# Edge layer of a four-layer network: VectorE's rows as max(c, -a) + a, and 8 of every 14 rows summed by TensorE in PSUM

## The chip, the cores and the metric

The kernel runs on one core of a Trainium2 chip. The metric is device time in microseconds (us); the median of three runs of the kernel before was 13131.24 us (13127.69 to 13149.08). The mean granted TensorE clock is read from the profile of each run, where 1.00 is full speed.

## The reference, cut to what matters

The program normalises and passes four samples through four residual layers: attention and an MLP, an edge layer, a spectral operator block, a convolution. The change concerns the second.

```python
def _L1_conv_ref(x, We, be, Wn, bn):        # x: [4 samples, 56 rows l, 56 n, 128 channels]
    W1, W2 = (We[:, :f], We[:, f:])
    proj_i = jnp.einsum('blnf,of->blno', x, W1)
    proj_j = jnp.einsum('blnf,of->blno', x, W2)
    edge = jax.nn.relu(proj_i[:, :, :, None, :] + proj_j[:, :, None, :, :] + be)
    edge_sum = edge.sum(axis=3)
    node_in = jnp.concatenate([x, edge_sum], axis=-1)
    node = jax.nn.relu(jnp.einsum('blnc,oc->blno', node_in, Wn) + bn)
    return node
# ...
x = x + _L1_conv_ref(_gn(x), We, be, Wn, bn)
```

With a = W1 n + be and c = W2 m, each row l needs a table of 56 x 56 = 3136 values relu(a[n] + c[m]) in each of 128 channels, summed over m. Everything is fp32.

## The kernel before

Channels lie on the partitions. Tiles lie in on-chip memory: in SBUF or, where TensorE's results go, in PSUM. A block is 8 rows; GpSimd builds the tables of the odd rows, VectorE those of the even ones, ScalarE applies the ReLU, and VectorE sums every row. VectorE takes c from PSUM (`pj3`), GpSimd from SBUF.

```python
        for j in range(NBLK):                       # 7 blocks of 8 rows
            # ... matmuls with W1 and W2; a = W1 xg + be and c = W2 xg go to SBUF, pj keeps c in PSUM
            pj3 = pj[:, :NB].rearrange("p (l n) -> p l n", l=8)
            for l in range(8):
                e = wk.tile([P, HH, HH], F32, name="e_e", bufs=4)
                if l % 2:
                    nc.gpsimd.tensor_add(e, bc(a[:, l, :], 2, HH), bc(c[:, l, :], 1, HH))
                else:
                    nc.vector.tensor_add(e, bc(a[:, l, :], 2, HH), bc(pj3[:, l, :], 1, HH))
                nc.scalar.activation(e, e, AF.Relu)
                nc.vector.tensor_reduce(es_[:, 8 * j + l, :], e, AX.X, ALU.add)
            # ... po = Wn[0] xg + Wn[1] es_ in PSUM; o = relu(po + bn) on ScalarE
            nc.vector.tensor_add(xf[:, blk(j)], xf[:, blk(j)], o)
```

`bc(t, axis, n)` repeats t n times along a new axis. After the edge layer, each sample is stored to memory (`x2d`), and the spectral layer loads it again as `s_x`, transposed. The first work of the spectral layer on a loaded sample is a group norm, then `s_xn`.

Of the kernel before, what the change touches and what calls it, by code (L numbers as in the profile page):

```python
# [11 lines left out]
F32 = mybir.dt.float32  # L12
# [19 lines left out]
def bc(ap, axis, n):  # L32
    """ap with a new axis of n repeats."""
    ap = ap.unsqueeze(axis)
    shape = list(ap.shape)
    shape[axis] = n
    return ap.to_broadcast(shape)
# [6 lines left out]
class Env:  # L44
    """What every phase shares: the context and the constants that stay on chip."""


def host_constants():
    """Constants of the shapes alone."""
# [33 lines left out]
def l0_host(i):  # L83
    """Layer 0's weights, laid out."""
# [32 lines left out]
def window_order(x):  # L117
    """[B, 56, 56, C] -> [B, C, 3136], tokens of the shifted windows one after another."""
    x = np.roll(x, (-3, -3), (1, 2)).reshape(B, 8, 7, 8, 7, P)
    return x.transpose(0, 5, 1, 3, 2, 4).reshape(B, P, TOK)  # L120


def group_norm_stats(k, pool, psum, xt, tag):
    """Mean and 1/sqrt(var + eps) of xt [128, 3136]'s groups of 4 partitions, as [128, 1] each."""
# [25 lines left out]
def layer_norm(k, pool, psum, src, dst, g, be):  # L150
    """Layer norm over the partitions (channels) of src [128, 3136] into dst."""
# [22 lines left out]
def evac(k, i, out, ps, bias):  # L174
    """PSUM plus a per-partition bias to SBUF, on ScalarE or VectorE by turns."""
# [13 lines left out]
def window_attention(k, w, xw, xf):  # L189
    """Attention inside the 7x7 windows of the normed xw [128, 3136] (window order) -> xf."""  # L190
# [64 lines left out]
def global_attention(k, w, xf):  # L255
    """xf += attention over all tokens of layer_norm(xf), xf [128, 3136]."""
    nc, tc = k.nc, k.tc
    scale = 1.0 / math.sqrt(32.0)
    with ExitStack() as es:
# [6 lines left out]
        # Head 2p + i has rows 64i .. 64i + 31 of ka[:, p] and qa[:, p, i]; row 64i + 32 is 1 in ka, the  # L266
        # shift in qa. qa's other rows are 0, so that a matmul takes both heads' rows and keeps one's.
# [14 lines left out]
        # 32 columns of a head's values, then 32 of ones, which add up the softmax's denominator.  # L282
# [54 lines left out]
def mlp(k, w, xf, xw, x1):  # L337
    """x1 (image order) = xw + xf + MLP(layer_norm(xf)); xw and xf in window order."""
# [30 lines left out]
def edge_layer(k, w, x1):  # L369
    """x1 += relu(Wn [n, sum over m of relu(W1 n + W2 m + be)] + bn) on the normed rows, x1 [128, 56, 56]."""  # L370
    nc, tc = k.nc, k.tc
    xf = x1.rearrange("p l n -> p (l n)")
    with ExitStack() as es:
        big = es.enter_context(tc.tile_pool(name="e_big", bufs=1))
        wk = es.enter_context(tc.tile_pool(name="e_wk", bufs=2))
        psum = es.enter_context(tc.tile_pool(name="e_ps", bufs=2, space=PSUM))
        mr = group_norm_stats(k, wk, psum, xf, "g")
        xg = big.tile([P, TOK], F32, name="e_xg")
        apply_norm(k, xg, xf, mr)
        es_ = big.tile([P, HH, HH], F32, name="e_sum")  # L380
        esf = es_.rearrange("p l n -> p (l n)")
        for j in range(NBLK):
            pi = psum.tile([P, 512], F32, tag="pi", name="e_pi")
            nc.tensor.matmul(pi[:, :NB], w.W1, xg[:, blk(j)], start=True, stop=True)
            a = wk.tile([P, 8, HH], F32, name="e_a")
            nc.scalar.activation(a.rearrange("p l n -> p (l n)"), pi[:, :NB], AF.Identity, bias=w.be)
            pj = psum.tile([P, 512], F32, tag="pj", name="e_pj")
            nc.tensor.matmul(pj[:, :NB], w.W2, xg[:, blk(j)], start=True, stop=True)  # L388
            c = wk.tile([P, 8, HH], F32, name="e_c")
            nc.scalar.copy(c.rearrange("p l n -> p (l n)"), pj[:, :NB])  # L390
            pj3 = pj[:, :NB].rearrange("p (l n) -> p l n", l=8)
            for l in range(8):
                e = wk.tile([P, HH, HH], F32, name="e_e", bufs=4)
                if l % 2:
                    nc.gpsimd.tensor_add(e, bc(a[:, l, :], 2, HH), bc(c[:, l, :], 1, HH))  # L395
                else:
                    nc.vector.tensor_add(e, bc(a[:, l, :], 2, HH), bc(pj3[:, l, :], 1, HH))  # L397
                nc.scalar.activation(e, e, AF.Relu)  # L398
                nc.vector.tensor_reduce(es_[:, 8 * j + l, :], e, AX.X, ALU.add)  # L399
            po = psum.tile([P, 512], F32, tag="mm", name="e_po")  # L400
            nc.tensor.matmul(po[:, :NB], w.Wn[:, 0, :], xg[:, blk(j)], start=True, stop=False)
# [552 lines left out]
```

## Time and profile before

| | before |
|---|---|
| median of 3 runs | 13131.24 us |
| span of the profiled run | 13125.1 us |
| mean granted TensorE clock | 0.803 |
| one edge stage (normed rows to last output add), four of them | 304.7 us |
| of it VectorE busy | 296.4 us |
| last output add of the edge layer to first `s_xn` | 8.2 us |
| from there to the end | 3700.8 us |

The page's first part for the kernel before (engine, busy us, share of the span, instructions) shows TensorE (PE) in front and VectorE (DVE) second:

```profile
PE 9832.7 (75%) x38858; PEld 4305.4 (33%) x38858; DVE 6024.5 (46%) x5577; ACT 2924.0 (22%) x3032; POOL 2708.8 (21%) x759
```

These shares average over stages with different limits. What counts for this change is which engine is never idle inside the edge stage; the prediction reads that.

### The profile page before, as it was taken

How to read it: one execution, taken by the hardware profiler on the slowest of the kernel's cores; microseconds unless marked ns; L12 is line 12 of the kernel's file. 1: busy time of each engine (PE TensorE's matmuls, PEld its weight loads, DVE VectorE, ACT ScalarE, POOL GpSimd, SP SyncE). 2: the span in 40 equal slices, each digit the busy share in tenths (PEclk: the TensorE clock that was granted, in tenths of full speed). 3: DMA queues.
4: the chain of work that ended last, by engine and by line, in shares of the span. 5: the costliest groups of instructions: out<-in, count | busy, mean ns of one | idle time of the engine just before them, and what ended most of it. 6: DMA issues, size and time to landing. Idle time of an engine off the chain costs nothing.

```text
span 13125.1 us, 90658 instructions
## 1 busy us (share of the span) xinstructions
PE 9832.7 (75%) x38858; PEld 4305.4 (33%) x38858; DVE 6024.5 (46%) x5577; ACT 2924.0 (22%) x3032; POOL 2708.8 (21%) x759
## 2 busy tenths in 40 slices
PE   7999993599999449999963999997252277654444
PEld 3333331233333123333321333332142266643332
DVE  5515317660441667135057622604848755533333
ACT  1031235203113430321343023034410000011111
POOL 1000003200000330000024000001337788831111
PEclk8999996699999669999975999998565555555555
DMA  0000000000000000000000000000000010100000
GB/s 15 0 0 0 0 0 5 5 0 0 0 0 0 5 5 0 0 0 0 0 0 5 0 0 0 0 0 10 22 4 1 6 25 23 25 8 10 10 10 5
DMA packets 17237, 68.42 MB, mean 5 GB/s; under 512 B 8154, under 2 KB 9994, under 8 KB 14146
## 3 DMA queue, kind: packets, MB, share of 16 engines
q1 hardware_dynamic: 16834, 62.62, 1.6%
q8 instruction: 305, 5.00, 0.2%
q14 instruction: 98, 0.80, 0.0%
HBM read 49.31 MB, written 13.30 MB: 5 GB/s over the span
## 4 chain that ended last, share of the span: by engine, by line
PE 71%; DVE 19%; POOL 4%; issue 3%; ACT 3%; DMA 0%; SPq 0%; POOLq 0%; DVEq 0%; ACTq 0%
PE a_p L300 21%; PE a_ss L318 20%; PE a_po L322 11%; PE u_po L766 6%; DVE e_sum L399 6%; DVE e_e L397 3%; DVE q_q L699 2%; POOL q_q L698 1%; DVE q_a L692 1%; PE id_pw L565 1%; PE id_pv L560 1%; DVE q_a L696 1%; PE sc_ps L580 1%; PE w_pt L242 1%; PE o_pk L801 1%
## 5 line engine op out<-in xcount | busy, mean ns | idle before, releaser
L318 PE MATMUL a_ss<-a_qa,a_ka 97*112 97x448 f32 x6272 | 2760.6, 562 | 0.0
L300 PE MATMUL a_p<-a_ka,a_qa 97*112 97x448 f32 x6272 | 2714.3, 565 | 21.7 <-DVE a_mx L301 21.2
L301 DVE TENSOR_REDUCE a_mx<-a_p 112x1 f32<-112x448 f32 x3136 | 1958.9, 625 | 1005.3 <-PE a_p L300 811.2
L320 ACT ACTIVATE a_pT<-a_ss 112x896 f32<-112x896 f32 x1568 | 1437.9, 917 | 2533.5 <-PE a_ss L318 2532.2
L327 DVE RECIPROCAL a_rec<-a_po 32x448 f32<-32x448 f32 x112 | 331.2, 2957 | 3172.6 <-PE a_po L322 3170.9
L363 POOL TENSOR_TENSOR x<-xf,xw 128x343 f32<-128x343 f32 (+2 forms) x36 | 29.9, 830 | 7490.2 <-DVE xf L357 7490.2
L318 PEld LDWEIGHTS a_ss<-a_qa,a_ka 97*112 97x112 f32 x6272 | 978.3, 176 | 1716.7 <-issue 1716.7
L322 PE MATMUL a_po<-a_pT,a_va 112*64 112x448 f32 x6272 | 1536.1, 564 | 0.0
L300 PEld LDWEIGHTS a_p<-a_ka,a_qa 97*112 97x112 f32 x6272 | 856.0, 175 | 1877.2 <-DVE a_mx L301 1862.9
L766 PE MATMUL u_po<-AT,u_u 112*112 112x56 f32 x4096 | 778.7, 393 | 347.8 <-DVE u_u L763 327.3
L766 PEld LDWEIGHTS u_po<-AT,u_u 112*112 112x112 f32 x4096 | 769.4, 306 | 357.1 <-issue 336.4
L399 DVE TENSOR_REDUCE e_sum<-e_e 128x56 f32<-128x3136 f32 x224 | 749.7, 3406 | 6.7 <-ACT e_e L398 6.7
L395 POOL TENSOR_TENSOR e_e<-e_a,e_c 128x3136 f32<-128x3136 f32 x112 | 610.0, 5448 | 576.6 <-DVE e_sum L399 521.8
L398 ACT ACTIVATE e_e<-e_e 128x3136 f32<-128x3136 f32 x224 | 621.0, 2810 | 283.4 <-POOL e_e L395 187.0
L762 POOL TENSOR_TENSOR u_v<-xh,u_d 112x1792 f32<-112x1792 f32 x128 | 671.1, 5264 | 16.2 <-issue 16.2
L322 PEld LDWEIGHTS a_po<-a_pT,a_va 112*64 112x64 f32 x6272 | 312.2, 134 | 1037.2 <-ACT a_pT L320 550.3
L184 ACT COPY a_qa<-a_pr 1x448 f32<-1x448 f32 x56 | 29.4, 524 | 2785.3 <-PE a_pr L309 2785.0
L761 DVE TENSOR_TENSOR u_u<-xh,u_d 112x1792 f32<-112x1792 f32 x128 | 395.0, 3088 | 463.5 <-PE u_po L766 449.9
L388 PE MATMUL e_pj<-e_xg,t_w_W 128*128 128x448 f32 x56 | 47.7, 952 | 494.7 <-DVE e_e L397 494.7
L402 PE MATMUL e_po<-e_sum,t_w_Wn 128*128 128x448 f32 x56 | 52.1, 1033 | 471.0 <-DVE e_sum L399 471.0
L704 PE MATMUL q_pp<-q_q,c_sym 128*128 128x112 f32 x64 | 23.7, 474 | 496.6 <-DVE q_q L699 496.6
L397 DVE TENSOR_TENSOR e_e<-e_a,e_pj 128x3136 f32<-128x3136 f32 x112 | 379.2, 3408 | 16.0 <-ACT e_c L390 16.0
(271 smaller groups left out, 8115.7 us busy)
## 6 DMA issues: line engine op xcount, KB each, us to landing
u_d<-dd SPq DMA_DIRECT2D x64, 392.0 KB
xw<-in_x SPq DMA_DIRECT2D x4, 1568.0 KB
x2d<-x SPq DMA_DIRECT2D x4, 1568.0 KB
s_x<-x2d SPq DMA_DIRECT2D x4, 1568.0 KB
o_x<-x2d SPq DMA_DIRECT2D x4, 1568.0 KB
out<-v_y SPq DMA_DIRECT2D x4, 1568.0 KB
t_w_qk<-in_w_qk SPq DMA_DIRECT2D x1, 1024.0 KB
t_w_w<-in_w_w SPq DMA_DIRECT2D x2, 256.0 KB
```

The costliest lines, as they stand in the source:

```text
L300: nc.tensor.matmul(pm[:KC, :NB], qa[rows, p, i, cs], ka[rows, p, blk(j)], start=True, stop=True)
L301: nc.vector.tensor_reduce(mx7[:, c, i, j:j + 1], pm[:KC, :NB], AX.X, ALU.max)
L318: nc.tensor.matmul(ss[:, i, :NB], ka[rows, p, cs], qa[rows, p, i, blk(j)], start=True, stop=True)
L320: nc.scalar.activation(pT, ss[:, :, :NB], AF.Exp, scale=scale)
L322: nc.tensor.matmul(po[64 * i:64 * i + 64, :NB], va[:, c, 2 * p + i, :], pT[:, i, :], start=(c == 0), stop=(c == NKC - 1))
L395: nc.gpsimd.tensor_add(e, bc(a[:, l, :], 2, HH), bc(c[:, l, :], 1, HH))
L397: nc.vector.tensor_add(e, bc(a[:, l, :], 2, HH), bc(pj3[:, l, :], 1, HH))
L398: nc.scalar.activation(e, e, AF.Relu)
L399: nc.vector.tensor_reduce(es_[:, 8 * j + l, :], e, AX.X, ALU.add)
L761: nc.vector.tensor_mul(u, x, bc(d[:, :, 0, :], 2, 2))
L762: nc.gpsimd.tensor_mul(v, x, bc(d[:, :, 1, :], 2, 2))
L766: nc.tensor.matmul(po[:112, b * HH:(b + 1) * HH], u[:, hp].rearrange("p i r -> p (i r)"), st.AT[:, hp, b, :], start=(hp == 0), stop=(hp == ...
```

## The change

The identity relu(a + c) = max(c, -a) + a lets the max take over the ReLU, and the sum over m of "+ a" is 56 a, which one small matmul with -56 Wn adds (na is -a). For 8 of every 14 rows nobody sums over m: TensorE multiplies each m column of the table by Wn and accumulates all 56 in the PSUM buffer of the output. VectorE builds six of those eight rows by max, GpSimd two by subtraction; the other six rows stay as they were, but all on GpSimd. Also, -a and c are now made for a whole sample ahead of its groups of 14 rows and kept in SBUF, so that the max takes both its inputs from there. The intent is to relieve VectorE and to use TensorE, which idles in this layer.

```diff
-            for l in range(8):
-                e = wk.tile([P, HH, HH], F32, name="e_e", bufs=4)
-                ...  # add on GpSimd or VectorE, ReLU, sum
+        for g0 in range(0, HH, G):                  # G, GP, GM, MQ = 14, 8, 6, 14
+            ...
+            nc.tensor.matmul(po[:, :GP * HH], w.Wn[:, 0, :], xg[:, sa], start=True, stop=False)
+            nc.tensor.matmul(po[:, :GM * HH], w56, na...[g0 rows], start=False, stop=False)
+            for m0 in range(0, HH, MQ):
+                e8 = wk.tile([P, GP, MQ, HH], F32, name="e_e8", bufs=3)
+                for lo, hi in ((0, GM), (GM, GP)):
+                    cb = bc(c[:, rows, m0:m0 + MQ], 3, HH)
+                    nb = bc(na[:, rows, :], 2, MQ)
+                    if lo == 0:
+                        nc.vector.tensor_tensor(e8[:, lo:hi], cb, nb, ALU.max)
+                    else:
+                        nc.gpsimd.tensor_sub(e8[:, lo:hi], cb, nb)
+                        ...  # ReLU on ScalarE
+                for m in range(MQ):
+                    nc.tensor.matmul(po..., w.Wn[:, 1, :], e8[:, :, m, :], start=False, stop=(m0 + m == HH - 1))
+                for _ in range(1 if m0 % (2 * MQ) == 0 else 2):
+                    e = wk.tile([P, HH, HH], F32, name="e_e")        # two buffers
+                    nc.gpsimd.tensor_sub(e, bc(c[:, row, :], 1, HH), bc(na[:, row, :], 2, HH))
+                    ...  # ReLU, VectorE's sum
```

More of the change, by code (lines that the diff above doesn't have):

```diff
@@ L44 @@
 class Env:
+    pass
 def host_constants():
@@ L372, in edge_layer @@
     xf = x1.rearrange("p l n -> p (l n)")
+    G, GP, GM, MQ = 14, 8, 6, 14
     with ExitStack() as es:
@@ L376, in edge_layer @@
         psum = es.enter_context(tc.tile_pool(name="e_ps", bufs=2, space=PSUM))
+        w56 = wk.tile([P, P], F32, name="e_w56", bufs=1)
+        nc.vector.tensor_scalar_mul(w56, w.Wn[:, 1, :], -float(HH))
         mr = group_norm_stats(k, wk, psum, xf, "g")
@@ L379, in edge_layer @@
         apply_norm(k, xg, xf, mr)
-        es_ = big.tile([P, HH, HH], F32, name="e_sum")
-        esf = es_.rearrange("p l n -> p (l n)")
+        na = big.tile([P, HH, HH], F32, name="e_na")
+        c = big.tile([P, HH, HH], F32, name="e_c")
         for j in range(NBLK):
@@ L384, in edge_layer @@
             nc.tensor.matmul(pi[:, :NB], w.W1, xg[:, blk(j)], start=True, stop=True)
-            a = wk.tile([P, 8, HH], F32, name="e_a")
-            nc.scalar.activation(a.rearrange("p l n -> p (l n)"), pi[:, :NB], AF.Identity, bias=w.be)
-            pj = psum.tile([P, 512], F32, tag="pj", name="e_pj")
+            nc.vector.tensor_scalar(na.rearrange("p l n -> p (l n)")[:, blk(j)], pi[:, :NB], w.be, -1.0, ALU.add, ALU.mult)
+            pj = psum.tile([P, 512], F32, tag="pi", name="e_pj")
@@ L388, in edge_layer @@
             nc.tensor.matmul(pj[:, :NB], w.W2, xg[:, blk(j)], start=True, stop=True)
-            c = wk.tile([P, 8, HH], F32, name="e_c")
-            nc.scalar.copy(c.rearrange("p l n -> p (l n)"), pj[:, :NB])
-            pj3 = pj[:, :NB].rearrange("p (l n) -> p l n", l=8)
-            for l in range(8):
-                e = wk.tile([P, HH, HH], F32, name="e_e", bufs=4)
-                if l % 2:
-                    nc.gpsimd.tensor_add(e, bc(a[:, l, :], 2, HH), bc(c[:, l, :], 1, HH))
-                else:
-                    nc.vector.tensor_add(e, bc(a[:, l, :], 2, HH), bc(pj3[:, l, :], 1, HH))
-                nc.scalar.activation(e, e, AF.Relu)
-                nc.vector.tensor_reduce(es_[:, 8 * j + l, :], e, AX.X, ALU.add)
@@ L400, in edge_layer @@
-            po = psum.tile([P, 512], F32, tag="mm", name="e_po")
-            nc.tensor.matmul(po[:, :NB], w.Wn[:, 0, :], xg[:, blk(j)], start=True, stop=False)
-            nc.tensor.matmul(po[:, :NB], w.Wn[:, 1, :], esf[:, blk(j)], start=False, stop=True)
-            o = wk.tile([P, NB], F32, name="e_o")
-            nc.scalar.activation(o, po[:, :NB], AF.Relu, bias=w.bn)
-            nc.vector.tensor_add(xf[:, blk(j)], xf[:, blk(j)], o)
+            nc.scalar.copy(c.rearrange("p l n -> p (l n)")[:, blk(j)], pj[:, :NB])
@@ new lines, in edge_layer @@
+        for g0 in range(0, HH, G):
+            po = psum.tile([P, 512], F32, tag="mm", name="e_po")
+            sa = slice(g0 * HH, (g0 + GP) * HH)
+            nc.tensor.matmul(po[:, :GP * HH], w.Wn[:, 0, :], xg[:, sa], start=True, stop=False)
+            nc.tensor.matmul(po[:, :GM * HH], w56, na.rearrange("p l n -> p (l n)")[:, g0 * HH:(g0 + GM) * HH],
+                             start=False, stop=False)
+            es_ = wk.tile([P, G - GP, HH], F32, name="e_sum")
+            row = g0 + GP
+            for m0 in range(0, HH, MQ):
+                e8 = wk.tile([P, GP, MQ, HH], F32, name="e_e8", bufs=3)
+                for lo, hi in ((0, GM), (GM, GP)):
+                    rows = slice(g0 + lo, g0 + hi)
+                    cb = bc(c[:, rows, m0:m0 + MQ], 3, HH)
[4 more added lines that the diff above has]
+                        nc.gpsimd.tensor_sub(e8[:, lo:hi], cb, nb)
+                        ef = e8[:, lo:hi].rearrange("p l m n -> p (l m n)")
+                        nc.scalar.activation(ef, ef, AF.Relu)
+                for m in range(MQ):
+                    nc.tensor.matmul(po[:, :GP * HH].rearrange("p (l n) -> p l n", l=GP), w.Wn[:, 1, :], e8[:, :, m, :],
+                                     start=False, stop=(m0 + m == HH - 1))
+                for _ in range(1 if m0 % (2 * MQ) == 0 else 2):
+                    e = wk.tile([P, HH, HH], F32, name="e_e")
+                    nc.gpsimd.tensor_sub(e, bc(c[:, row, :], 1, HH), bc(na[:, row, :], 2, HH))
+                    nc.scalar.activation(e, e, AF.Relu)
+                    nc.vector.tensor_reduce(es_[:, row - g0 - GP, :], e, AX.X, ALU.add)
+                    row += 1
+            po2 = psum.tile([P, 512], F32, tag="mm", name="e_po2")
+            sb = slice((g0 + GP) * HH, (g0 + G) * HH)
+            n2 = (G - GP) * HH
+            nc.tensor.matmul(po2[:, :n2], w.Wn[:, 0, :], xg[:, sb], start=True, stop=False)
+            nc.tensor.matmul(po2[:, :n2], w.Wn[:, 1, :], es_.rearrange("p l n -> p (l n)"), start=False, stop=True)
+            for ps, s in ((po, sa), (po2, sb)):
+                n = s.stop - s.start
+                o = wk.tile([P, GP * HH], F32, name="e_o")
+                nc.scalar.activation(o[:, :n], ps[:, :n], AF.Relu, bias=w.bn)
+                nc.vector.tensor_add(xf[:, s], xf[:, s], o[:, :n])
```

## The prediction

> **What bounds the kernel now.** I read the page first, for its engine shares and its chain of waits, then the timeline of the edge layer, then every engine's busy time inside that layer. The change touches nothing else: against the kernel before, the order of instructions on every engine is the same outside the edge layer, except that some BATCH_NORM_STATS2 just ahead of it move. So the question is what the four edge stages (one per sample) are worth, and what sets their pace.
>
> ```profile
> PE 71%; DVE 19%; POOL 4%; issue 3%; ACT 3%; DMA 0%; SPq 0%; POOLq 0%; DVEq 0%; ACTq 0%
> ...
> L399 DVE TENSOR_REDUCE e_sum<-e_e 128x56 f32<-128x3136 f32 x224 | 749.7, 3406 | 6.7 <-ACT e_e L398 6.7
> L395 POOL TENSOR_TENSOR e_e<-e_a,e_c 128x3136 f32<-128x3136 f32 x112 | 610.0, 5448 | 576.6 <-DVE e_sum L399 521.8
> L398 ACT ACTIVATE e_e<-e_e 128x3136 f32<-128x3136 f32 x224 | 621.0, 2810 | 283.4 <-POOL e_e L395 187.0
> ...
> L397 DVE TENSOR_TENSOR e_e<-e_a,e_pj 128x3136 f32<-128x3136 f32 x112 | 379.2, 3408 | 16.0 <-ACT e_c L390 16.0
> ```
>
> The first line is the chain that ended last, the others are groups of the edge layer: TensorE carries 71% of the whole kernel (global attention, untouched), VectorE 19%. In the edge layer VectorE is idle for 6.7 + 16.0 us in all, while GpSimd waits 521.8 us for VectorE's sums and ScalarE 283.4 us. VectorE is the bound there. The busy times of the four stages agree (columns: stretch; its length, then busy us and instructions of PE, PEld, DVE, ACT, POOL; then the granted clock):
>
> ```profile
> 2065.10:2369.80 304.70, 45.23 (x56) 13.77 (x56) 296.42 (x91) 166.11 (x77) 152.49 (x28) 0.51 0.00 0
> ```
>
> A stage lasts 304.7 us from the normed rows to the last output add, of which VectorE is busy 296.4. Four take 1219 us, 9.3% of the 13131 us. Eight rows repeat every 42.6 us (a VectorE sum starts at 2097.48 and the same one of the next block at 2140.11), so 14 rows cost 74.6 us.
>
> **A lock between VectorE and GpSimd.** I then asked what the new VectorE instructions collide with, because the old ones took care not to: L397 reads its second input from PSUM (e_pj). Two other places show what happens when both inputs lie in SBUF. The first is the output add of the edge layer itself, the second the score stage.
>
> ```profile
> 2110.79 3.42 DVE L397 TENSOR_TENSOR e_e<-e_a,e_pj 128x3136 f32<-128x3136 f32 x1
> 2114.12 2.77 DVE L405 TENSOR_TENSOR x<-x,e_o 128x448 f32<-128x448 f32 x1
> ...
> 2110.96 5.45 POOL L395 TENSOR_TENSOR e_e<-e_a,e_c 128x3136 f32<-128x3136 f32 x1 [1.21 <-DVE e_sum L399]
> ```
> ```profile
> 9753.85 5.20 DVE L692 TENSOR_TENSOR q_a<-S,t_w_qk 128x1792 f32<-128x1792 f32 x1
> ...
> 9753.21 3.96 POOL L698 TENSOR_TENSOR q_q<-q_a,q_c 128x1792 f32<-128x1792 f32 x1 [2.15 <-DVE q_a L696]
> 9757.24 4.85 POOL L694 TENSOR_TENSOR q_c<-iS,t_w_qk 128x1792 f32<-128x1792 f32 x1
> ```
>
> L397 (one input in PSUM) runs its usual 3.4 us under a GpSimd add. L405, which takes 0.62 us alone (its minimum), takes 2.77: it ends at 2116.89, just 0.48 us after the GpSimd add ends at 2116.41. L692 takes 2.01 us alone and 5.20 here, ending 1.88 us after GpSimd's 9757.17; then GpSimd's L694 (3.19 alone) takes 4.85, waiting for VectorE in turn. So the two exclude each other for whole instructions, less some 0.14 us of overlap at each change of hands, and a VectorE instruction that is waiting gets its turn before the next GpSimd one.
>
> **What the Trainium skill says.** SBUF — State Buffer, section "Who interferes with whom", says the same: a VectorE instruction with two SBUF inputs contends with a GpSimd one that reads SBUF, the later one blocks fully, while tensor_reduce and instructions with one SBUF input do not. The trace agrees (L399 stays at 3.40 to 3.42 us under GpSimd's adds). VectorE: DVE Perf Modes, section "The TRN2 errata", gives (N+151)/0.96 ns for an fp32 tensor_tensor: 3.42 us for 3136 elements, against 3.41 measured. FP8 and Floating Point Precision, section "TensorE Precision Notes", says true fp32 takes four passes; the trace shows each matmul as two MATMUL records. TensorE: Matmul & The Clock Gate, section "What's actually happening", says that the clock is halved after an idle window of some 3.4 us and comes back after a busy one. Here the stage starts at clock 0.52 (2065.0 to 2068.8) with records 0.75 us apart, then 1.00 with records 0.375 us apart.
>
> **The change, part by part.** It works in groups of 14 rows, 16 groups in all. Per group:
>
> Removed: all seven VectorE adds (3.41 each), seven of GpSimd's, 8 of 14 sums. VectorE had 7 x 3.41 + 14 x 3.41 = 71.6 us of these two kinds.
>
> VectorE now: four max of 6 x 14 x 56 = 4704 elements, (4704+151)/0.96 = 5.06 us each (estimate from the formula; the step from 1792 at 2.01 to 3136 at 3.41 gives 5.04), 20.2 us. Six sums at 3.41 are 20.4. Two output adds at 0.62 and 0.51, 1.1. Sum 41.8, plus in the first group the evacuation of na.
>
> GpSimd: six rows at 5.445, 32.7; four subtractions of 1568 elements at 2.81 (L232 has that size, also with one operand repeated along its innermost axis), 11.2. Sum 43.9.
>
> ScalarE: 6 x 2.81 + 4 x 1.5 + two output ReLUs, some 24 us: no bound.
>
> TensorE: 56 matmuls of 448 columns, 112 records at 0.375 us warm, 42.0 us, plus some 4 for the rest: 46. A quarter of 14 matmuls is 10.5 us warm. If it starts cold, the first 3.7 us do half work, so 12.4 us. Wholly cold it would be 21.
>
> If each engine ran by itself, a group would take some 47 us. But the max now reads c and na from SBUF. GpSimd's 43.9, the max's 20.2 and the output adds' 1.1 exclude each other: 65.2 us. There are six VectorE turns per group, so 12 changes of hands at 0.14 us of overlap, minus 1.7: 63.6. I walked two groups by hand in the issue order of the changed kernel (max, sum, max, sum, sum; sub, row, sub, row, row), a waiting VectorE instruction going first. The sums fall under GpSimd's rows, two row buffers are just enough, and the lock is almost never free; I add 1.0 us for the output adds, which hold VectorE behind a row. So 64.6 us per group, against 74.6. TensorE's quarter (12.4) fits into a quarter of the group (16.1), so TensorE is not on the path except at the end.
>
> One stage: 4.0 us to the first max (as to the first add now, 2065.12 to 2069.07), 4 x 64.6 = 258.4, less 1.1 for the last adds, plus a tail. The tail is new: the last quarter's ReLU 1.5, matmuls 12.4, then ReLU and add 1.6, so 15.5. In the kernel before it is 3.2 us after the last sum. That gives 276.8 against 304.7: 27.9 saved, 111.6 in four stages. The moved statistics: six of them (3.26 us) ran after the last GpSimd add ahead of each stage, now two are left, so some 2.1 us each, 8.5 in all. Total 120 us: 13131 - 120 = 13011.
>
> **Rivals.** (a) No lock in this form, for instance because the operands repeat an element. Then TensorE or GpSimd is the bound, some 50 us per group, a stage 4 + 200 + 15.5 = 219, 343 us saved, 12780 us, faster by 2.6%. For it: the split looks balanced for this (41.8, 43.9, 46). Against: L761 and L692 have repeated operands too and are blocked. (b) GpSimd holds the lock for several instructions on end. Then VectorE's sums come late behind the max, GpSimd waits for its two row buffers some 3.4 us a quarter, and a group takes 63.6 + 4 x 3.4 = 77: a stage some 326, 13210 us. For it: GpSimd's queue is always full. Against: L692 above got its turn. (c) TensorE stays cold: 4 x 21 = 84 us per group, a stage of 350, 13310 us. For it: the clock is 0.51 over the whole stage now, and the gaps of 3.7 us are near the window. Against: a cold quarter has no gap, and the clock came back within 3.7 us of work at 2068.8.
>
> **Range and chances.** The lock's sum is firm; idle time of the lock is not. One us per group is 16 us in the whole. From 60 to 68 us per group the time goes from 12935 to 13065; with some room for (b) and (c) I take 12930 to 13090. Faster by over 2% (below 12868) needs most of rival (a): 0.08. Slower by over 2% (above 13394) needs more than any rival gives: 0.02. The rest, 0.90, is within 2%.
>
> **What would show it.** Right: the max lasts far longer than 5.06 us in the mean (8 to 10), GpSimd's subtractions last longer than 5.445 and 2.81 (their busy time near 60 us a group or more), a group repeats every 64 to 65 us, TensorE's clock in the stage lies between 0.6 and 0.9, and a tail of 15 us follows the last subtraction. Wrong: max at 5.06 and a period near 50 (rival a), GpSimd idle for VectorE's sums (rival b), matmuls back to back at 0.75 us (rival c).

## The result

| | before | after |
|---|---|---|
| median, beside each other (4 runs each) | 13129.47 us | 13093.62 us |
| range | 13101.69 to 13149.08 | 13087.71 to 13098.3 |
| profiled span | 13125.1 us | 13096.5 us |
| one edge stage (the four lie within 0.5) | 304.7 us | 281.2 to 281.6 us |
| four stages | 1219.0 us | 1125.7 us |
| last output add to first `s_xn` | 8.2 us | 23.3 us |
| first `s_xn` to the end | 3700.8 us | 3756.8 us |

The ratio is 0.9972 (95% interval 0.9958 to 0.9987): the same within 2%, and 3.6 us above the predicted range. A ratio here and below is the mean time of one kernel's fast runs over that of the other's of the same rounds, so it is not quite the ratio of the medians quoted.

The page of the kernel after: the engines' busy times, then (cut) its chain that ended last, then groups of the edge layer (busy us, mean ns of one, idle time before them and what ended it).

```profile
PE 10533.2 (80%) x40666; PEld 4687.2 (36%) x40666; DVE 5660.3 (43%) x5437; ACT 2654.9 (20%) x2944; POOL 3088.2 (24%) x807
...
PE 73%; DVE 11%; POOL 8%; issue 5%; ACT 3%; DMA 0%; SPq 0%; POOLq 0%; DVEq 0%; ACTq 0%
...
L420 POOL TENSOR_TENSOR e_e<-e_c,e_na 128x3136 f32<-128x3136 f32 x96 | 658.0, 6868 | 55.9 <-DVE e_sum L422 55.9
L410 DVE TENSOR_TENSOR e_e<-e_c,e_na 128x4704 f32<-128x4704 f32 x64 | 439.2, 6862 | 5.5 <-ACT e_c L394 5.5
L422 DVE TENSOR_REDUCE e_sum<-e_e 128x56 f32<-128x3136 f32 x96 | 327.0, 3410 | 139.0 <-ACT e_e L421 139.0
```

VectorE fell by 364 us of busy time and its share of the chain from 19% to 11%, while GpSimd's (POOL) doubled from 4% to 8%. GpSimd's row, 5.45 us when nothing blocks it, lasts 6.87 in the mean. VectorE's sums, which have one input, last 3.41 as before. The max is best read by its spread, in the view of one source line (minimum, median and maximum in ns):

```profile
L410 DVE TENSOR_TENSOR e_e<-e_c,e_na x64: 5040/6928/10300, 2064.9 to 9290.8; 128x4704 f32<-128x4704 f32 x64
```

Its minimum of 5.04 us is close to the prediction's estimate of 5.06. The rest is waiting that the profile books as busy time, and the timeline of the first stage shows for what (start us, us, engine, line; in brackets idle time before it). VectorE first, then GpSimd, over the same stretch:

```profile
2177.01 6.97 DVE L410 TENSOR_TENSOR e_e<-e_c,e_na 128x4704 f32<-128x4704 f32 x1
2183.91 3.40 DVE L422 TENSOR_REDUCE e_sum<-e_e 128x56 f32<-128x3136 f32 x1
...
2198.29 6.89 DVE L410 TENSOR_TENSOR e_e<-e_c,e_na 128x4704 f32<-128x4704 f32 x1
...
2226.88 5.68 DVE L433 TENSOR_TENSOR x<-x,e_o 128x448 f32<-128x448 f32 x2 [8.16 <-ACT e_o L432]
```
```profile
2168.81 10.26 POOL L420 TENSOR_TENSOR e_e<-e_c,e_na 128x3136 f32<-128x3136 f32 x1
2179.03 7.63 POOL L412 TENSOR_TENSOR e_e<-e_c,e_na 128x1568 f32<-128x1568 f32 x1
2186.63 5.45 POOL L420 TENSOR_TENSOR e_e<-e_c,e_na 128x3136 f32<-128x3136 f32 x1
...
2194.81 15.68 POOL L420 TENSOR_TENSOR e_e<-e_c,e_na 128x3136 f32<-128x3136 f32 x2
...
2236.04 10.13 POOL L420 TENSOR_TENSOR e_e<-e_c,e_na 128x3136 f32<-128x3136 f32 x1 [4.38 <-DVE e_sum L422]
...
2318.78 7.63 POOL L412 TENSOR_TENSOR e_e<-e_c,e_na 128x1568 f32<-128x1568 f32 x1
```

The max begins at 2177.01, but GpSimd's row ends only at 2179.07 (2168.81 + 10.26); 5.04 us of work from there give 2184.1, and the max ends at 2183.98. GpSimd's small subtraction, 2.81 us by itself, begins at 2179.03 and ends at 2186.66, 2.68 us after the max: it did next to nothing while the max ran. The two rows at 2194.81 take 15.68 instead of 10.9 because the max of 2198.29 falls between them. Here the two engines alternate. At 2226.88 the output adds arrive late: VectorE has waited 8.16 us for their ReLU, then needs 5.68 us for 1.1 us of work because a GpSimd row is under way; the sum behind them is late, and GpSimd idles 4.38 us for it. The stage's last subtraction ends at 2326.41, and the stage at 2342.6, 16.2 us later.

Busy times of that stage (columns as in the prediction's view of before):

```profile
2060.90:2342.60 281.70, 204.62 (x508) 101.42 (x508) 207.49 (x56) 98.66 (x55) 247.40 (x40) 0.86 0.00 0
```

GpSimd shows 247 of 281.7 us, but its own work is 24 x 5.445 + 16 x 2.81 = 175.6; the 71.8 over that are waits. The granted clock is 0.86 against 0.51.

**What happened after the edge layer.** The rest of the table is outside it. The queue of DMA issues (SP) up to and just after the last output add, before (left out: constants) and after:

```profile
9018.38 0.79 SPq L599 DMA_DIRECT2D s_x<-x2d  x2
9416.17 0.32 SPq L906 DMA_DIRECT2D x2d<-x  x1
```
```profile
9316.50 0.32 SPq L934 DMA_DIRECT2D x2d<-x  x1
9316.92 0.37 SPq L627 DMA_DIRECT2D s_x<-x2d  x1
```

L599 and L627 are the same statement, as are L906 and L934. In the kernel before, two loads were issued (9018.38) long before the last one was stored (9416.17). In the kernel after, all four stores come first, and the first load is issued only when the edge layer is over. VectorE's timeline shows the price; before, then after:

```profile
9418.09 1.91 DVE L147 TENSOR_SCALAR s_x<-s_x,gn_mr 128x3136 f32<-128x3136 f32 x1
```
```profile
9326.66 3.79 DVE L128 BATCH_NORM_STATS2 gn_st<-s_x 128x6 f32<-128x448 f32 x7 [10.22 <-DMA s_x<-x2d]
```

Before, the sample was there and even its statistics were done: L147 applies them 2 us after the last add. After, VectorE waits 10.22 us for the load, then has the statistics still to do. That is the 15.1 us between 8.2 and 23.3.

The 56.0 us in the late part (3700.8 to 3756.8) come from short bursts of matmuls that ran at half the clock in one profile and at full clock in the other. The first image's burst is the plainest (windows over the burst, before and after; the last decimals are the granted clock):

```profile
9461.00:9482.00 21.00, 19.41 (x155) 15.46 (x153) 4.98 (x10) 4.02 (x9) 0.00 (x0) 1.00 0.00 1
```
```profile
9391.00:9422.00 31.00, 28.67 (x140) 26.04 (x138) 5.02 (x8) 3.10 (x7) 0.00 (x0) 0.50 0.00 1
```

The account of the two profiles: -93.3 (stages) - 6.4 (the layer starts earlier) + 15.1 (load) + 56.0 (late part) = -28.6, which is 13096.5 - 13125.1. How much of the 56 belongs to the change is a question for repeated runs.

### The profile page after: what moved, and what is told of

Its sections match the earlier page's. It is cut to its first block, busy times and chain, and to the rows that moved or that the text cites. A ratio compares the mean times of both kernels' runs of the same rounds, so it can differ in the third digit from the quotient of the medians.

```text
span 13096.5 us, 94238 instructions
## 1 busy us (share of the span) xinstructions
PE 10533.2 (80%) x40666; PEld 4687.2 (36%) x40666; DVE 5660.3 (43%) x5437; ACT 2654.9 (20%) x2944; POOL 3088.2 (24%) x807
## 4 chain that ended last, share of the span: by engine, by line
PE 73%; DVE 11%; POOL 8%; issue 5%; ACT 3%; DMA 0%; SPq 0%; POOLq 0%; DVEq 0%; ACTq 0%
PE a_p L300 21%; PE a_ss L318 20%; PE a_po L322 11%; PE u_po L794 6%; POOL e_e L420 3%; POOL e_e L412 2%; DVE q_q L727 2%; POOL q_q L726 1%; PE e_po L416 1%; DVE q_a L720 1%; PE id_pw L593 1%; PE sc_ps L608 1%; PE id_pv L588 1%; DVE q_a L724 1%; PE w_pt L242 1%
## 5 line engine op out<-in xcount | busy, mean ns | idle before, releaser
L416 PE MATMUL e_po<-e_e,t_w_Wn 128*128 128x448 f32 x1792 | 696.4, 549 | 17.6 <-ACT e_e L414 17.6
L420 POOL TENSOR_TENSOR e_e<-e_c,e_na 128x3136 f32<-128x3136 f32 x96 | 658.0, 6868 | 55.9 <-DVE e_sum L422 55.9
L416 PEld LDWEIGHTS e_po<-e_e,t_w_Wn 128*128 128x128 f32 x1792 | 349.0, 195 | 361.3 <-issue 339.8
L410 DVE TENSOR_TENSOR e_e<-e_c,e_na 128x4704 f32<-128x4704 f32 x64 | 439.2, 6862 | 5.5 <-ACT e_c L394 5.5
L422 DVE TENSOR_REDUCE e_sum<-e_e 128x56 f32<-128x3136 f32 x96 | 327.0, 3410 | 139.0 <-ACT e_e L421 139.0
L421 ACT ACTIVATE e_e<-e_e 128x3136 f32<-128x3136 f32 x96 | 270.5, 2817 | 481.1 <-POOL e_e L420 481.1
```

Source lines behind the costliest of these rows:

```text
L410: nc.vector.tensor_tensor(e8[:, lo:hi], cb, nb, ALU.max)
L416: nc.tensor.matmul(po[:, :GP * HH].rearrange("p (l n) -> p l n", l=GP), w.Wn[:, 1, :], e8[:, :, m, :], start=False, stop=(m0 + m == HH - 1))
L420: nc.gpsimd.tensor_sub(e, bc(c[:, row, :], 1, HH), bc(na[:, row, :], 2, HH))
```

## The experiments

The theory was that the lock sets the stage, that the load order costs 15 us, and that the late part is mostly chance; the rivals are stated with each run. All outputs were correct. The four stage times of one run never differ by more than 0.5 us, so a stage is given by one number.

**Both kernels again.** `before_again` is the kernel before and `after_again` the kernel after, both unchanged (no edit).

> The kernel before, once more, unchanged, for a second profile and for the spread of its times. Theory A (the late stages after the edge layer, which neither kernel changes, run some of their matmul bursts at full and some at half clock by chance from one execution to the next): the ratio to the kernel before is 1.000 with an interval of some +-0.2%, and this profile has another pattern of 12 us and 22 us bursts in the eight spectral convolutions than the first profile's 2 long ones of 8. Rival B (the pattern belongs to the kernel): again 2 long of 8, in the same places (third and eighth).

> The changed kernel, unchanged. Theory A (chance): the edge stages end 99 to 100 us earlier than before's as in the first profile, but the count of long convolution bursts differs from 5 of 8, and over more runs the median moves towards 13129 - 100 (edge stages with the statistics ahead of them) + 15 (the first load of the next stage is no longer issued early) = 13045. Rival B (the pattern belongs to the kernel): 5 long of 8 again and 13093 again.

Measured beside 11 runs of the kernel before (median 13144.25): 13145.23, ratio 0.9995 (0.9977 to 1.0012), and 13095.48, ratio 0.9958 (0.9942 to 0.9974). The change is worth 0.3% to 0.4%. Stages repeat to 0.1 us (304.8 and 281.6), as do 8.2 and 23.2; the late part was 3708.4 and 3734.3, so the difference there was now 26, not 56. For the kernel before, theory A came: three slow bursts at other places (fifth to seventh). For the kernel after it missed: five slow bursts again, though not the same five, and 13095 us instead of 13045, as rival B had it. These two runs alone therefore don't show chance.

**The lock undone: `psum`.** The max reads c from PSUM, freshly made by one more matmul per group; nothing else changes.

```diff
+            pc = psum.tile([P, 512], F32, tag="pc", name="e_pc")
+            nc.tensor.matmul(pc[:, :GM * HH], w.W2, xg[:, g0 * HH:(g0 + GM) * HH], start=True, stop=True)
+            pc3 = pc[:, :GM * HH].rearrange("p (l n) -> p l n", l=GM)
-                        nc.vector.tensor_tensor(e8[:, lo:hi], cb, nb, ALU.max)
+                        nc.vector.tensor_tensor(e8[:, lo:hi], bc(pc3[:, :, m0:m0 + MQ], 3, HH), nb, ALU.max)
```

> As the changed kernel, but the max reads c of its six rows from PSUM (one more matmul per group puts them there), so that it has only one input in SBUF. Lock theory: the max takes 5.06 us each (6.86 in the changed kernel), GpSimd's subtractions 5.45 and 2.81 (6.87 and 5.25), a group some 50 us instead of 64 to 72, an edge stage some 230 us instead of 281.6, and the whole some 190 us less than the changed kernel: about 12890. Rival (the stage is held by TensorE's 42 us of matmuls per group or by the in-order waits for the output ReLU, not by the lock): the durations fall but the group stays over 60 us and the whole is within 60 us of the changed kernel.

Measured: 12843.18 us (12836.08 to 12858.51), ratio 0.9769 (0.9752 to 0.9785), faster. A stage takes 224.6 us. Its groups, then its first stage:

```profile
L423 POOL TENSOR_TENSOR e_e<-e_c,e_na 128x3136 f32<-128x3136 f32 x96 | 523.7, 5464 | 81.9 <-DVE e_sum L425 81.8
...
L413 DVE TENSOR_TENSOR e_e<-e_pc,e_na 128x4704 f32<-128x4704 f32 x64 | 323.0, 5047 | 4.3 <-PE e_pc L403 4.3
```
```profile
2062.00:2286.70 224.70, 200.98 (x516) 100.86 (x516) 178.50 (x56) 98.57 (x55) 175.34 (x40) 0.95 0.00 0
```

The max lasts 5.05 in the mean instead of 6.86, GpSimd's row 5.46 instead of 6.87, though both engines do exactly the same work. The lock is shown: undoing it was worth 57 us a stage. The 224.6 lie near the 219 that rival (a) of the prediction gave to a kernel without it. Now TensorE is busy 201 of 224.7 us, at clock 0.95. This version beats both kernels and was not beaten by the ones below.

**Less GpSimd work: `gm8`.** VectorE makes all eight rows, GpSimd none of them. By lock arithmetic this should be shorter: 16 subtractions of 2.81 fall away per stage against 16 x (6.69 - 5.06) us of longer max (estimates from the formula of the prediction).

```diff
-    G, GP, GM, MQ = 14, 8, 6, 14
+    G, GP, GM, MQ = 14, 8, 8, 14
-                for lo, hi in ((0, GM), (GM, GP)):
+                for lo, hi in ((0, GM),):
```

> As the changed kernel, but VectorE makes the max of all eight rows and GpSimd none of them. Lock theory: what counts is the sum of both engines' locked time, 6 x 5.45 + 4 x 6.69 + 1.1 = 60.6 us per group instead of 65.3, so 16 x 4.7 = 75 us less than the changed kernel. If GpSimd's own work were the bound, 16 x 11.2 = 180 us less; if VectorE's own work were, 4 x 1.63 = 6.5 us per group more, 104 us more.

Measured: 13054.78 us (13041.09 to 13087.69), ratio 0.9932 (0.9912 to 0.9951), but a stage of 283.2, not shorter than 281.6. A miss. Its groups:

```profile
L420 POOL TENSOR_TENSOR e_e<-e_c,e_na 128x3136 f32<-128x3136 f32 x96 | 904.2, 9438 | 221.8 <-DVE e_sum L422 149.9 <-DVE e_na L391 71.9
...
L410 DVE TENSOR_TENSOR e_e<-e_c,e_na 128x6272 f32<-128x6272 f32 x64 | 470.7, 7355 | 5.2 <-ACT e_c L394 5.2
```

The max got its turn nearly at once (7.36 in the mean, 6.68 at the least), and GpSimd, blocked to 9.44 per row, also idled 149.9 us for VectorE's sums: when the lock's load is cut, something else ends the waits. The other timed runs (13041.09 to 13068.4) came out lower than the profiled one (13087.69). That one has six slow convolution bursts of eight, of some 10 us each (see the last experiment); whether the others had fewer is not shown, since only the profiled one has a trace.

**Is it the row buffers? `gm8_rows3`**. The same with three row buffers instead of two, paid for by two buffers instead of three for the pieces that TensorE sums.

```diff
-                e8 = wk.tile([P, GP, MQ, HH], F32, name="e_e8", bufs=3)
+                e8 = wk.tile([P, GP, MQ, HH], F32, name="e_e8", bufs=2)
-                    e = wk.tile([P, HH, HH], F32, name="e_e")
+                    e = wk.tile([P, HH, HH], F32, name="e_e", bufs=3)
```

> gm8 with three row buffers instead of two (and two instead of three buffers for the pieces that TensorE sums, so that it fits). In gm8 the locked work fell by 18 us per stage but the stage stayed (283.2 against 281.6 us), and GpSimd waited 150 us for VectorE's sums. If two row buffers, freed by sums that stand in VectorE's queue behind a blocked max, are why the lock stood free, the stage falls to 250 to 265 us. If something else holds it (VectorE's queue itself), it stays above 275.

Measured: 13049.45 us (13040.21 to 13072.86), ratio 0.994 (0.9923 to 0.9957), stage 275.7.

```profile
L420 POOL TENSOR_TENSOR e_e<-e_c,e_na 128x3136 f32<-128x3136 f32 x96 | 879.3, 9189 | 167.3 <-DVE e_sum L422 95.1 <-DVE e_na L391 72.3
...
L422 DVE TENSOR_REDUCE e_sum<-e_e 128x56 f32<-128x3136 f32 x96 | 324.9, 3408 | 12.3 <-ACT e_e L421 12.3
```

GpSimd's waits for sums fell from 149.9 to 95.1, so the row buffers were part of it, for 7.5 us a stage net of the piece buffer given up. But the stage stayed above the 275 at which the expectation called something else the cause. It points to VectorE's queue: VectorE idles only 12.3 us in all before its sums, and its max now lasts 8.98 us in the mean (6.68 at the least), so the sums come late behind a blocked max.

**The lock put into the kernel before: `before_sb`.** VectorE's add reads c from SBUF too.

```diff
-                    nc.vector.tensor_add(e, bc(a[:, l, :], 2, HH), bc(pj3[:, l, :], 1, HH))
+                    nc.vector.tensor_add(e, bc(a[:, l, :], 2, HH), bc(c[:, l, :], 1, HH))
```

> The kernel before with one operand changed: VectorE's adds read c from its copy in SBUF instead of from PSUM, so they have two SBUF inputs. Same instructions, same sizes. Lock theory: VectorE's adds and GpSimd's adds exclude each other; both are released by the same sum, so some two adds per block of eight rows wait out a GpSimd add of 5.45 us: 42.6 us per block becomes 48 to 55, 28 blocks, 150 to 350 us more in the whole (13280 to 13480). Without a lock: VectorE's add takes 3.43 instead of 3.41 us, nothing measurable.

Measured beside 9 runs of the kernel before (median 13146.65): 13179.89 us (13166.06 to 13198.61), ratio 1.0027 (1.0011 to 1.0042), stage 306.0. A miss: far less than expected.

```profile
L395 POOL TENSOR_TENSOR e_e<-e_a,e_c 128x3136 f32<-128x3136 f32 x112 | 954.7, 8526 | 262.5 <-DVE e_sum L399 207.8 <-ACT e_c L390 54.8
...
L397 DVE TENSOR_TENSOR e_e<-e_a,e_c 128x3136 f32<-128x3136 f32 x112 | 422.2, 3794 | 16.0 <-ACT e_c L390 16.0
```

The lock is there: GpSimd's adds went from 5.45 to 8.53 us. But it fell on GpSimd, because VectorE's add starts first where both are released together. Two lines of the timeline, VectorE's and GpSimd's:

```profile
2123.21 3.41 DVE L397 TENSOR_TENSOR e_e<-e_a,e_c 128x3136 f32<-128x3136 f32 x1
```
```profile
2123.36 8.56 POOL L395 TENSOR_TENSOR e_e<-e_a,e_c 128x3136 f32<-128x3136 f32 x1 [1.21 <-DVE e_sum L399]
```

VectorE is 0.15 us ahead and keeps its 3.41 us; GpSimd takes 8.56. And GpSimd had time to spare: its wait for sums shrank from 521.8 to 207.8 us. VectorE lost 43.0 us on its adds (422.2 less 379.2), but won 30 on its output adds (28 of them, 2.456 us in the mean before and 1.372 now) and the 6.7 us that it had waited before sums (now 0.0). What is left, some 6, is about what four stages are longer, 4.9. (The timed runs are 33 us longer in the medians. The profiled one has four slow convolution bursts and the slow first image in its late part, 3741.7 us; for the others that is not shown.) So a lock costs little where the blocked engine has slack. In the kernel after GpSimd has next to none: its idle time between its first and last instruction of the first stage is 14 us.

**The max alone: `max_only`.** The kernel before with max(c, -a) on VectorE's rows (c still from PSUM), no ReLU for them, and the small correcting matmul, but without summing on TensorE.

```diff
+            na = wk.tile([P, 4, HH], F32, name="e_na")
+            nc.vector.tensor_scalar_mul(na, a.rearrange("p (x i) n -> p x i n", i=2)[:, :, 0, :], -1.0)
-                    nc.vector.tensor_add(e, bc(a[:, l, :], 2, HH), bc(pj3[:, l, :], 1, HH))
-                nc.scalar.activation(e, e, AF.Relu)
+                    nc.vector.tensor_tensor(e, bc(na[:, l // 2, :], 2, HH), bc(pj3[:, l, :], 1, HH), ALU.max)
+                if l % 2:
+                    nc.scalar.activation(e, e, AF.Relu)
     # ... and w56 times na added into po
```

> Half of the change alone, in the kernel before: VectorE's rows are max(c, -a), c still read from PSUM, without their ReLU on ScalarE, and the missing 56 a is added by one more small matmul; all rows are still summed by VectorE. Both theories: VectorE has the same adds and sums and stays the bound at 42 to 43 us per block, ScalarE's work falls by 112 ReLUs (315 us of busy time) that nobody waited for. The whole changes by less than 30 us. If the ReLUs did sit on the path, it would fall by up to 100 us.

Measured: 13179.57 us (13149.25 to 13190.09), ratio 1.0022 (1.0008 to 1.0036), stage 312.6, 7.8 more than before. The max takes what the add took (3.41), and ScalarE, which it relieves, was never the bound. The loss lies in the new small instruction on VectorE that makes -a:

```profile
L390 DVE TENSOR_SCALAR e_na<-e_a 128x224 f32<-128x224 f32 x28 | 41.5, 1493 | 10.5 <-ACT e_a L388 10.5
```

In 12 of its 28 times it lasts 0.27 us; in the other 16 it falls under a GpSimd add, lasts 2.41 and ends 0.13 to 0.14 us after that add. It has one input, in SBUF, so here a VectorE instruction with a single SBUF input waited for GpSimd too; 16 x 2.14 = 34 us, and four stages are 31.3 longer. All the gain of the change therefore comes with the summing on TensorE and the new split of rows.

**Only more memory: `before_pad`.** The kernel before with one more row buffer, to test whether a larger edge layer alone loses the early load.

```diff
-                e = wk.tile([P, HH, HH], F32, name="e_e", bufs=4)
+                e = wk.tile([P, HH, HH], F32, name="e_e", bufs=5)
```

> The kernel before with a fifth row buffer in the edge layer, which VectorE as the bound can't use, but which takes the memory where the first image of the next stage would land: by the issue order that load now comes after the last store, as in the changed kernel. Theory: the edge stages stay at 304.7 us, the first subtraction of the next stage starts 23 us after the last edge output instead of 8, and the whole is 15 us (0.1%) longer. If the rest of the changed kernel's missing gain (some 36 us in the late stages) also comes from that load, it is 50 us longer.

Measured: 13097.27 us (13083.62 to 13117.32), ratio 0.9966 (0.9953 to 0.9978). The load is lost as the theory said (23.3 instead of 8.2 us). But the kernel is faster, which nobody expected: a stage takes 291.9 instead of 304.7. The view of the output add's line, before and in `before_pad`, shows why:

```profile
L405 DVE TENSOR_TENSOR x<-x,e_o x28: 624/2760/2771, 2114.1 to 9415.5; 128x448 f32<-128x448 f32 x28
```
```profile
L405 DVE TENSOR_TENSOR x<-x,e_o x28: 617/625/633, 2113.9 to 9360.2; 128x448 f32<-128x448 f32 x28
```

With one more buffer the add no longer falls under a GpSimd add. It took 2.456 us in the mean before (the line's busy time over 28), now 0.625: 28 x 1.83 = 51 us, and four stages are 51.5 us shorter. One collision, already visible in the kernel before, was worth about as much as the whole change brought.

**Two attempts to better `psum`.** `best` is `psum` with pieces of 7 columns of m instead of 14, so that TensorE starts sooner and ends sooner, and with PSUM buffers of its own for po and pj (one each for pj and for the c that the max reads; in `psum` the latter has two). `psum_po` (third call) has `psum` with only po's own buffers.

```diff
-    G, GP, GM, MQ = 14, 8, 6, 14
+    G, GP, GM, MQ = 14, 8, 6, 7         # best only; its rows spread over 8 pieces instead of 4
-            po = psum.tile([P, 512], F32, tag="mm", name="e_po")
+            po = psum.tile([P, 512], F32, tag="po", name="e_po")
```

> The kernel with c in PSUM (psum), with pieces of 7 instead of 14 columns, and own PSUM buffers for the accumulating output and for the two projections, so that TensorE doesn't wait 3 to 7 us between groups for the output ReLU and the projections don't queue behind each other. Theory: TensorE's 46 us per group is what is left: an edge stage of 4 + 4 x 47 + 12 = 204 us instead of psum's 224.7, so some 80 us less than psum, 12760. Rival: the in-order queues of VectorE and ScalarE hold it at psum's time.

> psum with one edit more: the accumulating output has its own two PSUM buffers instead of sharing two with the output of the other rows. In psum TensorE stands still 3 to 7 us between groups until the output ReLU has freed a buffer, and starts again at half clock. Theory: that wait goes, some 5 us for three group changes per stage, 60 us in the whole, 12780. Rival: the stage is held by the sums in VectorE's queue (GpSimd waited 81.8 us for them in psum) and nothing changes: 12843.

Measured: `best` 12919.55 us (12912.98 to 12927.57), ratio 0.9828 (0.9815 to 0.9842), stage 249.1; `psum_po` 12847.21 us (12836.94 to 12860.26), ratio 0.9779 (0.9766 to 0.9793), stage 228.1 against 224.6. Both missed. In `best`, GpSimd's small subtractions:

```profile
L415 POOL TENSOR_TENSOR e_e<-e_c,e_na 128x784 f32<-128x784 f32 x128 | 194.9, 1525 | 235.5 <-PE e_po L419 150.7 <-ACT e_c L394 42.5 <-issue 42.2
```

They wait 150.7 us for TensorE to free a piece, where `psum` waited 8.0. Three pieces of half the size hold half as much work between the engines, which would explain it; that was not tested by itself. Po's own buffers change little either way.

**First table first: `psum_first`**. `psum`, with the c of the first group made by the stage's first matmul.

```diff
+        first = c_of(0)                   # c_of(g0): the matmul and view of psum's edit
         for j in range(NBLK):
+            pc3 = c_of(g0) if g0 else first
```

> psum with the c of the first group made by the first matmul of the stage instead of after four blocks of projections. In psum the first max starts 10.5 us after the normed rows are there, against 4.0 in the changed kernel. Theory: the max starts at 4 to 5 us and the stage loses 4 to 6 of its 224.6 us, 20 us in the whole: 12825. Rival: the first group is held by the copies of c on ScalarE, and nothing changes.

Measured beside 7 runs of the kernel before (median 13133.44): 12878.77 us (12870.86 to 12895.23), ratio 0.9807 (0.9792 to 0.9822), stage 239.9. A miss: GpSimd's wait for TensorE's pieces rose to 63.4 us, as the same view shows, so VectorE did not start sooner to any use; why exactly the pieces come free later I did not follow up.

```profile
L419 POOL TENSOR_TENSOR e_e<-e_c,e_na 128x1568 f32<-128x1568 f32 x64 | 184.3, 2884 | 109.3 <-PE e_po L423 63.4 <-ACT e_c L400 45.8
```

**More profiles of the two kernels.** The late part was still open: 56 us more in the first pair of profiles, 26 in the second. `look_b1` and `look_b2` are the kernel before, `look_a1`, `look_a2` and `look_a3` the kernel after, one execution each (no edit).

> The kernel before unchanged, for another profile: how many of the eight spectral-convolution bursts run at half clock (22 us instead of 12)? Chance theory: any number from 1 to 6. If the pattern belongs to the kernel: 2 to 3, as in its two profiles so far.

> The changed kernel unchanged, for another profile. Chance theory: any number of long bursts from 1 to 6. If the pattern belongs to the kernel: 5, as in its two profiles so far.

> As look_b1, once more: the kernel before unchanged. Chance theory: 1 to 6 long bursts of eight; if the pattern belongs to the kernel: 2 to 3.

> The changed kernel unchanged, for another profile of its late stages. So far the stretch from the next stage's first subtraction to the end took 3757, 3734 and 3733 us here and 3701, 3708, 3711 and 3732 in the kernel before. Chance alone: 3700 to 3760, 1 to 6 long convolution bursts of eight. A lasting shift: again above 3730.

> The changed kernel unchanged, once more, for its late stages. Chance alone: 3700 to 3760 us from the next stage's first subtraction to the end. A lasting shift against the kernel before (mean 3713 of four): again above 3730.

Measured times: 13134.74 and 13156.09 (before), 13074.81, 13098.76 and 13081.86 (after). With the earlier profiles there are now four of before and five of after:

| | before, 4 profiles | after, 5 profiles |
|---|---|---|
| four stages, mean | 1219.0 | 1126.3 |
| edge layer ends at, mean | 9417.6 | 9321.2 |
| to first `s_xn` | 8.2 each time | 23.2 to 23.4 |
| late part | 3700.8, 3708.4, 3711.0, 3732.3 | 3756.8, 3734.3, 3732.9, 3747.1, 3736.5 |
| late part, mean | 3713.1 | 3741.5 |
| first image's bursts at half clock | 0 of 4 | 4 of 5 |
| spectral-convolution bursts at 22 instead of 12 us, of 8 | 2, 3, 3, 5 | 5, 5, 3, 2, 3 |

The late part differs by 28 us in the mean. The spectral-convolution bursts at half clock change their number and place between executions of one and the same program (13 of 32 against 18 of 40), so they are chance, some 10 us each. The first image's two bursts are not so evenly spread: at half clock they take some 22 us longer together. Over all twelve profiles whose load is late (those of `psum`, `gm8` and so on too) they were slow in six, over the six with an early load in one. That leans towards the late load shifting them, but does not settle it.

Counting slow bursts accounts for nearly all of the late part. Less 10 us for each slow convolution burst and 22 for each slow first or third image (the third was slow once, in `look_a2`), it is 3678 to 3682 us in the four profiles of before and 3681 to 3685 in the five of after. So of the 28 us in the mean, some 18 are the first image, 4 the third, 3 to 4 the convolution bursts, and 3 are left; of the 56 in the first pair, three bursts and the first image make 52.

## Why the prediction was right or wrong

**The lock was right.** That the max, with both inputs in SBUF, and GpSimd exclude each other was the step on which the forecast departed from rival (a), and `psum` shows it: one operand moved to PSUM, 57 us a stage. The max at its predicted length of 5.05 when free, a sum untouched at 3.41, the granted clock of 0.86 and the tail of 16.2 (15.5 said) are as the prediction's last paragraph asked. GpSimd is busy 247.4/4 = 61.9 us a group, as said. One sign was too strong: the max has a mean of 6.86, not 8 to 10, since GpSimd takes more of the waits (71.8 us a stage, against 16 x (6.86 - 5.05) = 29 in the max). The hand-walked order was good enough, but not in every group: the first stage's groups begin 69.2, 64.2 and 67.1 us apart, against 64 to 65. One reading left something out: VectorE idled not 6.7 + 16.0 us before, but 10.5 more ahead of its output adds; the bound is the same.

**One term was too small: "I add 1.0 us for the output adds".** The stage took 281.6 against 276.8. The first max started 4.0 us in, as said. From there to the end of the last subtraction the prediction had 258.4 - 1.1 = 257.3 us, and 261.5 were measured; the tail adds 0.7. Most of the missing 4.2 us are idle time of the lock. In that stretch neither a GpSimd instruction nor a max or output add is under way for 7.3 us in all, where the prediction allowed 4 x 1.0. Of it 3.3 and 3.5 us lie in the two waits of 4.38 and 8.81 us in which GpSimd stood for a sum. In the first the sum was behind output adds whose ReLU came late; in the second it was behind a max that had itself waited for GpSimd. In the sum, 1.0 us per group is to be replaced by 7.3/4 = 1.8; what remains, about 1 us a stage, is that changes of hands overlapped less than was allowed (an estimate: it is what the sum leaves). Over four stages it cost 18 us: 93.3 saved, not 111.6.

**The statistics were about right:** from GpSimd's last add ahead of a stage to the normed rows it took 9.58 us before and 6.8 to 7.0 after, 10.7 us less in four stages, 8.5 said (one of the moved instructions is left there, not two). All that lies ahead of and between the stages took 6.4 us less in the first pair (8190.7 against 8197.1), but that stretch varies by 13 us between profiles of the kernel before and by 9 in the kernel after.

**The wrong step was "The change touches nothing else".** I had compared the order of instructions on the engines, and not asked when the DMA queue may start. The early load of `s_x` was lost, which cost 15.1 us in each of the five profiles, and in `before_pad` by nothing but one more buffer of 12.5 KB a partition (3136 x 4 bytes). That it is the memory that the edge layer's larger tiles hold until the end is an inference from that run; the trace does not show addresses. The DMA queue's own waits agree: with the early load (in `before`, `before_sb` and `max_only`) it was released by an instruction of the global attention (`a_pf`, L333, after 1951 to 1953 us), as if it landed where that layer's tiles had lain; in `after`, `psum` and `before_pad` no load waits for that one. On top of it, the late part was longer by 28 us in the mean and by 56 in the first pair. A part of that is chance of the clock, for which my range had no room: it was drawn from the time per group alone. Where the first image's bursts are slow they add some 22 us, 18 in the mean of the five, and whether the late load causes that is open.

In the first pair of profiles, the 120 us foretold become 28.6 by 18.3 (stages), 2.1 (ahead of and between them), 15.1 (load) and 56.0 (late part), which is 91.5 within rounding. In the means of four and five profiles it is 52.9: the layer ends 96.4 earlier, less 15.1 and 28.4.

**The rivals.** (b) is seen in small: GpSimd does wait for sums, 55.9 us in all, at the ends of groups rather than in every quarter. (c) did not come: the clock rose. (a) is what the change would have been with one operand in PSUM. The chances put 0.90 on within 2%, which came; the range was too narrow, because it allowed for the time per group and not for the rest of the kernel.

**Where the gain went.** Without the lock, moving the sums to TensorE shortens a stage by 80 us (304.7 to 224.6 in `psum`). The change as made kept 23 of them; 57 went into the lock that comes with reading c from SBUF. Of the 93 us left in four stages, 15 were then given back to the late load and 28 in the mean (56 in the first pair) in the late part, some 18 of these in the first image's bursts.

## What to carry to other kernels

Before two engines are given balanced shares, ask which of their operands lie in SBUF: here a VectorE tensor_tensor with two of them was added to GpSimd's time, not laid beside it, and one operand in PSUM undid that. A scalar multiplication with its one input in SBUF waited too (`max_only`), so look at each instruction's spread of times. What a lock costs depends on which engine is made to wait and whether it has slack. And when a change alters the memory that a phase holds, look at what the next phase had loaded early.

## What the Trainium skill lacked or had wrong

- SBUF — State Buffer, section "Who interferes with whom", says that issue order decides who blocks, and the runs agree: with VectorE's add 0.15 us ahead of GpSimd's, `before_sb` put the wait on GpSimd (8.53 us per add instead of 5.45) more than on VectorE (3.79 instead of 3.41). For two such instructions it lacks the change of hands: VectorE's add ends 0.48 us after GpSimd's though it takes 0.62 alone, and with both queues full the two took turns in the kernel after.
- GPSIMD Engine Reference, section "3.1 Elementwise — side-by-side cycle accounting", gives some 2.6 cycles per element, 4497 ns for 2048 elements, for a two-input operation. A plain one here agrees (6.81 us for 3136, 2.17 ns each). It lacks that the edge layer's form, with operands repeated along an axis, is cheaper: 5.45 us for 3136, 1.74 ns each.
- TensorE: Matmul & The Clock Gate lacks how far a short burst late in a program, beyond a kernel's first matmuls, varies between executions of that program. Spectral-convolution bursts took 12 or 22 us by chance, in 2 to 5 of 8 cases, which makes up to some 30 us between two executions here, nearly as much as the whole change brought.
